# Edge attention on one core: the order of two matmuls, E and Q, in each batch of edges

## The chip, the cores and the metric

The kernel runs on one core of a Trainium2 chip. The time is the device time in microseconds (us) of one execution. The engines are named as in the profile: PE is TensorE (PEld its weight loads), DVE is VectorE, ACT is ScalarE, POOL is GpSimd and SP is the queue that issues plain transfers. They run side by side, each in the order of its own queue, and wait for each other through semaphores.

## The reference

A graph has 6250 nodes with 128 features each (8 heads of 16), and 206250 directed edges, sorted by destination node. Each edge has 128 features of its own.

```python
Qh, Kh, Vh = h @ WQ, h @ WK, h @ WV          # per node, seen as (N, 8, 16)
Eh = edge_attr @ WE                          # per edge
score = einsum('ehd,ehd,ehd->eh', Kh[src], Qh[dst], Eh) / sqrt(16)
score = exp(clip(score, -5, 5))
wV = segment_sum(Vh[src] * score[:, :, None], dst)
Z  = segment_sum(score, dst)
out = layernorm(x + wV / (Z[:, :, None] + 1e-6))
```

So every edge needs K and V of its source node, Q of its destination node and its own E.

## The kernel before

The edges are cut into 1612 tiles of 128, and the tiles into 406 batches: 401 of four tiles, and five small ones at the end. A short first part builds a table of K and V for all nodes in HBM (`kv`). The first 12 batches don't use it: they gather rows of x and project them themselves (`project`).

For each tile POOL issues one indirect DMA, which gathers 128 rows of 256 numbers (K and V of the sources) into `kvrows` (`gather`, L308 to L324). There are 15 buffers of one batch each. From batch 16 on, the first gather of a batch also waits for a matmul: `add_manual_dep` (L318 to L323) ties it to `expanded[b - lag(b)]`, which is the Q matmul of an earlier batch. The lag is 12 batches at first and falls by one every four batches to 1, which it reaches at batch 60 (L304 to L306).

Q of the destinations isn't gathered. Since the edges are sorted, a tile's destinations lie in a short window of nodes, and Q is spread to the edges by a matmul with a one-hot matrix (`qw`, in bfloat16 parts, times `onehotT`) into the PSUM tile `qps`. E comes from a float32 matmul of `we_sb` with the edge features `ea` into the PSUM tile `eps`. Both stand in `stage_a`. ACT copies `qps` to `qT` in SBUF, and DVE multiplies `qT` with `eps` to `eq` (`pairs`, L368). The PSUM pools of E and Q have one buffer each.

The stages of a batch are spread over several turns of the main loop (L481 to L533). In turn b the queues get, in this order:

- POOL: the gathers of batch b.
- PE: the four transposes of `eq` of batch b-1 into `pps` (`turn`, L376), then Q and E of batch b (`stage_a`), sometimes a block of nodes to finish (L412, L416), then `agg` of batch b-3 (`stage_c`, L441), sometimes a block of Q rows (L259).
- ACT: the copy of Q of batch b (L359), then the two exponentials of batch b-2 (L394, L396).
- DVE: `kq` of batch b-2 (L382, which needs its gathers landed), its reduction (L385) and clip (L388), `msg` of batch b-3 (L423), the one-hot matrices of batch b+2 (L343, L347), and `eq` of batch b (L368). Small operations of the layer norm are put between them (`fill`).
- SP: edge features (L295), destination rows (L285), windows of Q (L278), stores.

Until batch 12 the framework's scheduler orders the instructions. From batch 12 on the order is that of the code (`manual_schedule`, L482). At batch 60 the edges inside their windows are counted (L529, `count_inside`, with one small matmul, L200).

Of the kernel before, what the change touches and what calls it, by code (L numbers as in the profile page):

```python
# [8 lines left out]
F32 = mybir.dt.float32  # L9
# [6 lines left out]
P = 128  # L16
# [9 lines left out]
B = 4  # L26
# [54 lines left out]
def edge_attention(ctx: ExitStack, tc: tile.TileContext, x, xT, srcT, dstT, dstB, dst0, bnd, lo, eaT,  # L81
                   wq, wkv, we, out, kv, qtab, qs, relD):
    nc = tc.nc
# [14 lines left out]
    we_sb = cp.tile([D, D], F32, name="we_sb")  # L98
# [13 lines left out]
    with ExitStack() as fast:  # L112
# [94 lines left out]
        psE = fast.enter_context(tc.tile_pool(name="psE", bufs=1, space=bass.MemoryType.PSUM))  # L207
# [82 lines left out]
        def load_chunk(c):  # L290
            if c in chunks or c * CH >= NT:
                return
            n = min(CH, NT - c * CH) * P
            tl = ep.tile([P, CH * P], F32, name="ea")
            nc.sync.dma_start(tl[:, :n], eaT[:, c * CH * P:c * CH * P + n])  # L295
            chunks[c] = tl

        def ea_tiles(t, n):

            load_chunk(t // CH)  # L300
            j = t % CH * P
            return chunks[t // CH][:, j:j + n * P]
# [23 lines left out]
        def project(g, n):  # L326

            pt = psT.tile([P, B, P], F32, name="xtps", tag="oT")
            for i in range(n):
                nc.tensor.transpose(pt[:, i, :], g[:, i, :D], ident)  # L330
            xgT = wp.tile([P, B, P], F32, name="xgT", tag="kq", bufs=2)
            nc.scalar.copy(xgT[:, :n], pt[:, :n])
            for i in range(0, n, 2):
                k = min(2, n - i)
                pk = pair_bank(i // 2, "kvps", [P, 2, 2 * D])
                for j in range(k):
                    nc.tensor.matmul(pk[:, j, :], xgT[:, i + j, :], wkv_sb, start=True, stop=True)
                nc.scalar.copy(g[:, i:i + k, :], pk[:, :k, :])  # L338
# [12 lines left out]
        def stage_a(b, g):  # L351
            t0, n = batches[b][0], len(batches[b])
            if b < XB:
                project(g, n)
            oh, ohT = st8.pop(b)
            pq = psQ.tile([P, B * P], F32, name="qps")
            expanded[b] = nc.tensor.matmul(pq[:, :n * P], loaded[t0 // WT], ohT[:, :n * P], start=True, stop=True)  # L357
            qT = wp.tile([P, B * P], F32, name="qT", bufs=2)
            nc.scalar.copy(qT[:, :n * P], pq[:, :n * P])  # L359
            pe = psE.tile([P, B * P], F32, name="eps")  # L360
            nc.tensor.matmul(pe[:, :n * P], we_sb, ea_tiles(t0, n), start=True, stop=True)  # L361
            st8[b] = [n, g, oh, pe, qT]

        def pairs(b):
# [116 lines left out]
        for b in range(nbat + 4):  # L481
# [6 lines left out]
            if b < nbat:  # L488
                load_chunk(batches[b][0] // CH + EB - 3)
                load_rel(batches[b][0] // RC + 1)  # L490
                load_q(batches[b][0] // WT + QLOOK)
                g = gathered.pop(b) if b in gathered else gather(b)
                if b == min(XB, nbat - 1):
                    late_loads()
                if b == min(XB + 8, nbat - 1):
                    relative(C0, NT)
                if b == 14:
                    from_window(1)
                if b == 0:
                    for i in range(AHEAD):  # L500
                        stage_0(i)
                if b > 0:
                    turn(b - 1)
                stage_a(b, g)
            elif b == nbat:
                turn(b - 1)
# [184 lines left out]
```

## Time and profile before

| | us |
|---|---|
| median of 4 runs (lowest, highest) | 2044.31 (2042.33, 2045.83) |
| the profiled execution | 2045.63 |
| its span, first to last instruction | 2043.8 |
| busy in the span: PE, PEld | 1425.6, 993.9 |
| busy in the span: DVE, ACT, POOL | 1563.9, 473.7, 1533.3 |
| mean granted clock of TensorE | 0.886 |
| gathers on POOL: 1612, of which 1564 from the table | 0.951 each |

The profile comes from one execution. Its page has the busy time of each engine, the span in slices, the chain of work that ended last, and the costliest groups of instructions: line, engine, operation, output and inputs, count, then the total busy time and the mean of one in ns, then the idle time of the engine just ahead of them and what ended most of it. A timeline lists instructions in order: start in us, duration in us, engine, line and operation, and in brackets the idle time ahead of it with what ended it. Ends of matmuls are modelled, since they are pipelined. A float32 matmul shows as two rows (x2).

### The profile page before, as it was taken

What the parts mean: (1) busy time and instruction counts of PE and PEld (TensorE: products, weight loads), DVE (VectorE), ACT (ScalarE), POOL (GpSimd) and SP (SyncE); (2) the same over time, 40 slices, a digit from 0 to 9 for tenths busy, and PEclk for the clock granted to TensorE, in tenths of its full rate; (3) what the DMA queues carried; (4) which work ended last, traced back from release to release, by engine and by line L of the source; (5) the groups of instructions that cost most, each with busy time, mean ns of one, the idle gap of its engine ahead of it and who ended that gap; (6) DMA issues with size and microseconds to landing.
All of it is one profiled execution on the core that took longest, in us unless ns stands there. A gap on an engine that the chain in (4) does not pass through costs nothing.

```text
span 2043.8 us, 24333 instructions
## 1 busy us (share of the span) xinstructions
PE 1425.6 (70%) x6736; PEld 993.9 (49%) x6736; DVE 1563.9 (77%) x3542; ACT 473.7 (23%) x1548; POOL 1533.3 (75%) x1619
## 2 busy tenths in 40 slices
PE   6877876675767677766677676766776667666765
PEld 4655554453544445544444454544554444444444
DVE  3689998777778768777777777777878678777776
ACT  2422222222222222222222222221222222222221
POOL 7777777777777777777777777777777777777775
PEclk9989998989888988888888888888878888988888
DMA  9776766657666675656665666667565765666652
GB/s 297 226 229 194 226 197 212 195 174 211 192 196 184 186 212 171 205 174 190 210 189 174 199 203 197 183 188 217 167 201 174 207 203 179 195 182 199 202 169 81
DMA packets 177711, 398.12 MB, mean 195 GB/s; under 512 B 60988, under 2 KB 86758, under 8 KB 177568
## 3 DMA queue, kind: packets, MB, share of 16 engines
q0 software_dynamic: 76592, 208.18, 34.6%
q1 hardware_dynamic: 99836, 187.38, 29.3%
q8 instruction: 56, 0.92, 0.2%
q10 hardware_dynamic: 1140, 0.93, 0.1%
q14 instruction: 87, 0.71, 0.1%
HBM read 381.54 MB, written 14.81 MB: 194 GB/s over the span
## 4 chain that ended last, share of the span: by engine, by line
DMA 32%; DVE 26%; POOL 17%; issue 13%; PE 11%; ACT 1%; DVEq 0%; ACTq 0%; POOLq 0%; SPq 0%
DMA kvrows<-kv,src 30%; POOL kvrows L315 17%; DVE kq L382 7%; DVE sc L385 6%; PE agg L441 4%; DVE msg L423 3%; DVE eq L368 3%; PE eps L361 2%; DVE onehot L343 2%; PE pps L376 2%; DVE onehotT L347 1%; DVE sc L388 1%; DMA kv<-kvst 1%; PE finps L412 1%; PE qps L357 1%
## 5 line engine op out<-in xcount | busy, mean ns | idle before, releaser
L315 POOL DMA_INDIRECT kvrows<-kv,src x1564 | 1486.8, 951 | 478.1 <-issue 368.6
L441 PE MATMUL agg<-msg,onehot 128*128 128x136 f32 x3224 | 536.4, 316 | 518.4 <-DVE msg L423 420.9
L441 PEld LDWEIGHTS agg<-msg,onehot 128*128 128x128 f32 x3224 | 475.1, 217 | 833.7 <-issue 662.8
L382 DVE TENSOR_TENSOR kq<-kvrows,pps 128x512 f32<-128x512 f32 x406 | 275.5, 679 | 348.9 <-DMA kvrows<-kv,src 345.4
L361 PE MATMUL eps<-ea,we_sb 128*128 128x512 f32 (+1 forms) x812 | 469.5, 662 | 0.7 <-ACT kvrows L338 0.7
L359 ACT COPY qT<-qps 128x512 f32<-128x512 f32 x406 | 236.3, 582 | 540.7 <-PE qps L357 538.7
L376 PE MATMUL pps<-shift,eq 128*128 128x128 f32 x1612 | 299.7, 316 | 62.3 <-DVE eq L368 58.8
L368 DVE TENSOR_TENSOR eq<-qT,eps 128x512 f32<-128x512 f32 x406 | 272.9, 672 | 22.3 <-PE eps L361 19.7
L385 DVE TENSOR_REDUCE sc<-kq 128x32 f32<-128x512 f32 x406 | 276.0, 680 | 9.0
L423 DVE TENSOR_TENSOR msg<-kvrows,bank 128x512 f32<-128x512 f32 x406 | 274.1, 675 | 5.3 <-ACT bank L394 5.3
L343 DVE TENSOR_TENSOR onehot<-bank,dst_sb 128x512 f32<-128x512 f32 x406 | 274.5, 677 | 0.0
L394 ACT ACTIVATE bank<-sc 128x32 f32<-128x32 f32 x406 | 81.8, 201 | 822.5 <-DVE onehot L343 812.9
L376 PEld LDWEIGHTS pps<-shift,eq 128*128 128x128 f32 x1612 | 207.6, 159 | 118.9 <-DVE eq L368 114.1
L361 PEld LDWEIGHTS eps<-ea,we_sb 128*128 128x128 f32 x812 | 178.4, 221 | 28.6 <-ACT kvrows L338 3.4
L357 PE MATMUL qps<-onehotT,qw 126*128 126x512 bf16 x406 | 176.1, 434 | 0.9 <-ACT qT L359 0.9
L347 DVE TENSOR_SCALAR onehotT<-relb,node 126x512 bf16<-126x512 bf16 x406 | 152.4, 376 | 7.7 <-DMA relb<-relD 4.5
L388 DVE TENSOR_SCALAR sc<-sc 128x32 f32<-128x32 f32 x406 | 89.2, 220 | 9.0
L396 ACT ACTIVATE msg<-sc 128x32 f32<-128x32 f32 x406 | 86.6, 213 | 0.2
L315 POOL DMA_INDIRECT kvrows<-x,src x48 | 45.6, 951 | 16.4 <-issue 12.2
L454 ACT COPY sum<-agg 128x136 f32<-128x136 f32 x146 | 38.6, 265 | 35.6 <-PE agg L441 33.8
L357 PEld LDWEIGHTS <-qw 126*128 126x128 bf16 x406 | 44.5, 110 | 1.1 <-issue 0.9
L232 PE MATMUL kvacc<-wkv_sb,xT_sb 128*128 128x256 f32 (+1 forms) x98 | 29.3, 458 | 13.1 <-DMA xT_sb<-xT 5.4
(69 smaller groups left out, 474.3 us busy)
## 6 DMA issues: line engine op xcount, KB each, us to landing
ea<-eaT SPq DMA_DIRECT2D x201, 512.0 KB
relb<-relD SPq DMA_DIRECT2D x100, 504.0 KB
kvrows<-kv,src POOLq DMA_INDIRECT x1564
qw<-qs SPq DMA_DIRECT2D x202, 31.5 KB
kv<-kvst SPq DMA_DIRECT2D x12, 512.0 KB
qs<-qst SPq DMA_DIRECT2D x48, 96.0 KB
xb<-x SPq DMA_DIRECT2D x24, 128.0 KB
out<-h SPq DMA_DIRECT2D x24, 128.0 KB
```

Source lines behind the costliest of these rows:

```text
L315: ins = nc.gpsimd.indirect_dma_start(out=g[:k, i, :f], out_offset=None, in_=rows, in_offset=bass.IndirectOffsetOnAxis(ap=src_col(t)[:k], a ...
L343: nc.vector.tensor_tensor(oh[:, :n], iota_p[:, None, :].to_broadcast([P, n, P]), rel[:, t0:t0 + n, None].to_broadcast([P, n, P]), op=ALU.i ...
L347: nc.vector.tensor_scalar(ohT[:, :n * P], rels[t0 // RC][:, e0:e0 + n * P], node[:QROWS], None, op0=ALU.is_equal)
L357: expanded[b] = nc.tensor.matmul(pq[:, :n * P], loaded[t0 // WT], ohT[:, :n * P], start=True, stop=True)
L359: nc.scalar.copy(qT[:, :n * P], pq[:, :n * P])
L361: nc.tensor.matmul(pe[:, :n * P], we_sb, ea_tiles(t0, n), start=True, stop=True)
L368: nc.vector.tensor_tensor(eq[:, :n * P], qT[:, :n * P], pe[:, :n * P], op=ALU.mult)
L376: nc.tensor.transpose(pp[:, i, :], eq[:, i * P:i * P + P], ident)
L382: nc.vector.tensor_tensor(t1[:, :n], g[:, :n, :D], pp[:, :n], op=ALU.mult)
L385: nc.vector.tensor_reduce(sc[:, :n], t1[:, :n].rearrange("p b (h d) -> p b h d", h=H), axis=AX.X, op=ALU.add)
L423: nc.vector.tensor_tensor(m[:, :n, :D].rearrange("p b (h d) -> p b h d", h=H), g[:, :n, D:].rearrange("p b (h d) -> p b h d", h=H), exp_p[ ...
L441: nc.tensor.matmul(aggs[k], oh[:, i, :], m[:, i, :], start=first and not final, stop=last)
```

## The change

In `stage_a` the E matmul is issued ahead of the Q matmul instead of behind it. Nothing else differs. The copy of Q stays behind Q.

```diff
@@ stage_a
             oh, ohT = st8.pop(b)
+            pe = psE.tile([P, B * P], F32, name="eps")
+            nc.tensor.matmul(pe[:, :n * P], we_sb, ea_tiles(t0, n), start=True, stop=True)
             pq = psQ.tile([P, B * P], F32, name="qps")
             expanded[b] = nc.tensor.matmul(pq[:, :n * P], loaded[t0 // WT], ohT[:, :n * P], start=True, stop=True)
             qT = wp.tile([P, B * P], F32, name="qT", bufs=2)
             nc.scalar.copy(qT[:, :n * P], pq[:, :n * P])
-            pe = psE.tile([P, B * P], F32, name="eps")
-            nc.tensor.matmul(pe[:, :n * P], we_sb, ea_tiles(t0, n), start=True, stop=True)
             st8[b] = [n, g, oh, pe, qT]
```

With the lines moved, E is line 357, Q line 359 and the copy line 361 in the changed kernel; the others keep their numbers.

## The prediction

> **What bounds the kernel now.** I read the page from the top, and its first part misleads. No engine is over 77% busy, and the chain that ended last hops between DMA, DVE and POOL. So I went to the costliest groups, and asked of each what ended its idle time.
>
> ```profile
> PE 1425.6 (70%) x6736; PEld 993.9 (49%) x6736; DVE 1563.9 (77%) x3542; ACT 473.7 (23%) x1548; POOL 1533.3 (75%) x1619
> ...
> L315 POOL DMA_INDIRECT kvrows<-kv,src x1564 | 1486.8, 951 | 478.1 <-issue 368.6
> ...
> L382 DVE TENSOR_TENSOR kq<-kvrows,pps 128x512 f32<-128x512 f32 x406 | 275.5, 679 | 348.9 <-DMA kvrows<-kv,src 345.4
> ...
> L368 DVE TENSOR_TENSOR eq<-qT,eps 128x512 f32<-128x512 f32 x406 | 272.9, 672 | 22.3 <-PE eps L361 19.7
> ```
>
> The gather row tells it: 1564 gathers of 0.95 us with 478.1 us of idle time, which is 0.30 us for each. POOL therefore starts a gather every 1.25 us and does nothing else. The timeline of POOL alone confirms it: 1612 gathers run from 3.61 to 2027.51 us, 2023.9 us for 1611 steps, median step 1.25. Only 11.6 us of that lies above 1.25 per step. What follows the last gather (2027.5 to 2043.8, 16.3 us) is DVE's row of small operations and one store. So **POOL's stream of gathers is the kernel's clock**. DVE idles 345.4 us for gathers that have not landed. The wait the change is aimed at, DVE's product eq for TensorE's E (L361), is 19.7 us in 31 pieces on an engine with that much to spare.
>
> The one thread from the edit back to POOL is the pace wait (L318 to L325). From batch 16 on, the first gather of batch b waits for the Q matmul of batch b-lag(b); the lag falls from 12 to 1 at batch 60 and stays there. I set each batch's first gather beside the end of that Q matmul, from the timelines of POOL and PE. A gather that waits starts 0.28 us behind the end of Q. Two do so in this execution, batch 25 and batch 28. This is the first:
>
> ```profile
> 128.05 0.95 POOL L315 DMA_INDIRECT kvrows<-kv,src  x1 [0.30 <-issue]
> ...
> 129.49 0.63 PE L357 MATMUL qps<-onehotT,qw 126*128 126x512 bf16 x1
> ...
> 129.92 1.19 PE L361 MATMUL eps<-ea,we_sb 128*128 128x512 f32 x2
> ...
> 130.16 0.58 ACT L359 COPY qT<-qps 128x512 f32<-128x512 f32 x1 [2.58 <-PE qps L357]
> 130.40 0.94 POOL L315 DMA_INDIRECT kvrows<-kv,src  x1 [1.40 <-PE qps L357]
> ```
>
> Q of batch 15 ends at 130.12, E at 131.11 (129.92 + 1.19), and POOL starts batch 25 at 130.40, 1.1 us late. Time lost there is lost for good, since POOL never has room to catch up.
>
> **The change, part by part.** It removes and adds no instruction that computes. The built order of the two programs differs on PE only from batch 12 on (in the first 12 the scheduler puts E and Q in the same places), and there E stands ahead of Q. On DVE 394 products wait for ACT alone instead of PE and ACT. On SP 190 loads of edge features lose a wait on PE. ACT and POOL keep their order and their waits.
>
> *Freed wait on DVE.* The trace has 394 semaphore instructions of 21 ns ahead of eq, 8.3 us in all, on DVE's queue. Where DVE runs without a gap eq starts with no idle time ahead of it, so they are covered by the operation before. I take 0; the other end is ten batches between 15 and 25 at 21 ns, 0.2 us earlier.
>
> *Freed wait on SP.* E of a batch ended at most 1.7 us behind its Q, and a reload of Q's weights for the same batch still waits for that Q, which now ends last. The loads go out at the same time: 0. Q in turn now stands behind E's wait for its features; E sat idle 0.7 us in all, none of it for a load, so 0 again.
>
> *eq's operands.* Before, eq is ready when E ends (warm: Q's start + 1.24; the copy ends 0.24 earlier). After, the pair still takes 1.24 us, but the copy follows it: 0.04 to start and 0.58 to run. So eq is ready 0.6 us later than now. In a run of batches without a DMA wait eq starts 1.1 to 1.3 us after E's end, so 0.6 is hidden; 71 of 389 eq start within 0.75 us of it, and DVE loses up to 0.6 there. Behind a waiting eq stand kq, the reduction and msg of older batches, and behind msg TensorE's agg. So the wait that was removed is replaced by a longer one. Nearly all of it disappears into the 345.4 us for which DVE waits for gathers anyway.
>
> *The gather's release.* This is the part on the path. Q is now done when E was done: 0.86 us later in the median of batches 12 to 400, up to 1.72 where the clock was low. Subtracting that and 0.28 from the room of every first gather from batch 16, three of 390 turn clearly negative (batch 32 stands at 0.02, with what POOL lost before it to spare):
>
> - Batch 25 waits for Q of 15: Q ends at 131.11 instead of 130.12, **+0.99 us**.
> - Batch 28 waits for Q of 19, which ended at 145.45 and E at 146.31: 0.86 later by itself. It is later still by eq of batches 15 and 18, both of which started within 0.11 us of E's end and now wait some 0.5 us each for the copy. That is 1.4 to 1.9, of which 0.99 is already in POOL's stream: **+0.4 to +0.9**.
> - Batch 62 waits for Q of 61, which sits behind the counting of line 530:
>
> ```profile
> 316.72 0.63 PE L357 MATMUL qps<-onehotT,qw 126*128 126x512 bf16 x1
> ...
> 317.14 1.91 PE L361 MATMUL eps<-ea,we_sb 128*128 128x512 f32 x2
> ...
> 318.31 0.94 POOL L315 DMA_INDIRECT kvrows<-kv,src  x1 [0.30 <-DVE msg L423]
> ```
>
> Here Q ends at 317.35, E at 319.05, and the gather starts at 318.31. The gather would start at 319.05 + 0.28 = 319.33, **+1.02**. DVE had last waited for a gather at batch 57, so what POOL lost before shifts both sides alike.
>
> Unknown is whether E in front exposes its weight load: Q's takes 0.10, one of E's 0.2, so 0 to 0.1 us at each of the three, 0 to 0.3. Below nothing is excluded because the pair's matmuls are the same.
>
> After batch 63 the lag is one and the room is wide: counted with E already in front, its median is 5.6 us, its least inside the run 0.41 (batch 277). The last two batches have 0.66 and -0.01, which the shift of POOL's stream leaves about where it is. The tail hangs on kq at 2020.35, which waits for a gather, and shifts with it.
>
> Sum: 0.99 + 0.65 + 1.02 + 0.15 = **+2.8 us** (2.4 to 3.2). The profiled execution took 2045.63 us (span 2043.8), which gives 2048.4. The median of the four runs is 2044.31, 1.3 below that execution, so the median forecast is **2047.1 us**, +0.14%. This kernel's runs spread from 2042.33 to 2045.83, and a difference within 0.2% (4.1 us) is about what can't be told from none.
>
> [...] The rows show two lengths of the same matmul: Q 0.38 and 0.63 us, with E's end 0.86 and 1.70 behind it, and PEclk between 0.8 and 1.0. [...] With all three places slow the sum would be 3 x 1.70 = 5.1 us, an estimate, against 2.8 by the rows; I keep the rows, where one place was slow throughout, one in part, and one not.
>
> **Rivals.**
> 1. *It does nothing measurable for POOL* (0 to +1.5 us, 2044 to 2046). For it: 387 of 390 waits have room. It needs batches 15, 19 and 61 to fall better by luck. Against: batches 25 and 28 are at the wait already, so any lateness of Q there goes straight in. Chance 0.18.
> 2. *Slower: the pace wait binds in the steady state.* Place: the lag-one waits from batch 60. Mechanism: eq is late by 0.6 after a stall, then the transposes, then E and Q, and the lateness X reaches the next release on top of E. With X taken from the room of all 346 lag-one waits, the loss is 2.3 us at X = 0.5, 5.2 at 1.0, 11.7 at 1.5. Part of it is batch 62's own, 1.02 + X. With the 1.6 to 2.2 us of the ramp the total passes 4.1 from X of about 0.5, which is where it decides; the median would be 2051.4 at X = 1.0 and 2058 at 1.5. For it: 46 eq start within 0.2 us of E's end. Against: the narrow waits come right after a stall, where eq had been ready long before. Chance 0.20.
> 3. *Faster.* What POOL lost to Q is 1.1 us at batch 25 and 0.3 at 28. If the freed semaphore waits brought the ramp forward by all of it, the median would be 2042.9. I see no source for 4 us, since 2012 of 2044 us are POOL's own pitch. Chance of over 0.2% faster 0.03, of a smaller gain 0.04.
>
> **How the numbers follow.** The forecast (+1.5 to +4.1) has 0.55, rival 1 0.18, rival 2 0.20, rival 3 0.07 in its two parts. Faster by over 0.2% is 0.03, slower by over 0.2% 0.20, and the rest, 0.55 + 0.18 + 0.04, is 0.77. The range runs from 2043.3, which is rival 1's lower end less the scatter of a median, to 2052.0, which takes in rival 2 up to X of about 1.0; about 0.17 is left out.
>
> **What would show it.** In the profile after, POOL's mean gather stays at 951 ns with 0.30 us ahead of it. Gathers of batches 25, 28 and 62 show idle time put down to PE qps, and the last gather starts 2 to 3 us later. ACT's copy starts about 0.86 us later in each batch against the transposes. eq's idle time is put down to ACT's copy and is larger than 22 us, some 40 to 70, and DVE's wait for gathers is smaller by about as much. I am wrong if POOL's idle time rises over many batches past 60 (rival 2), or if POOL's last gather moves and none of the three places does.

## The result, and the profile after

The changed kernel takes 2046.63 us (median of 32 runs, 2042.41 to 2049.96), the kernel before 2044.43 us (52 runs, 2042.18 to 2047.50). The ratio is 1.0011, with a 95% interval of 1.0006 to 1.0015: slower by 1.2 to 3.1 us, clear of the noise, but inside the 0.2% that the prediction calls hard to tell from none. The forecast was 2047.1, +2.8 us. The profiled execution of the changed kernel took 2049.32 us, that of the kernel before 2045.63.

The page of the changed kernel, the lines that answer to those shown of before (line, engine, operation, count, then busy us, mean ns, idle us ahead and what ended most of it):

```profile
span 2047.5 us, 23810 instructions
...
PE 1428.0 (70%) x6736; PEld 954.1 (47%) x6736; DVE 1563.2 (76%) x3542; ACT 467.4 (23%) x1548; POOL 1532.8 (75%) x1619
...
L315 POOL DMA_INDIRECT kvrows<-kv,src x1564 | 1485.1, 950 | 482.6 <-issue 374.4
...
L382 DVE TENSOR_TENSOR kq<-kvrows,pps 128x512 f32<-128x512 f32 x406 | 275.3, 678 | 330.3 <-DMA kvrows<-kv,src 327.6
...
L368 DVE TENSOR_TENSOR eq<-qT,eps 128x512 f32<-128x512 f32 x406 | 273.1, 673 | 45.7 <-ACT qT L361 43.8
```

Two columns are to be compared. eq's idle time is now put down to the copy and is 43.8 us instead of 19.7 for E, and DVE's wait for gathers is 327.6 instead of 345.4: it fell by 17.8, so about three quarters of the 24.1 that eq waits longer were paid out of the old wait. And POOL's gathers cost the same (950 ns), but its idle time ahead of the table's gathers rose from 478.1 to 482.6 us. That 4.5 is what POOL lost in this execution by waiting. The span rose by less, 3.7 us (2043.8 to 2047.5), since the gathers themselves took 0.5 us less in all and the work behind the last one 0.3 less. POOL's timeline says where the waiting lies. The gathers of batches 25, 28, 32 and 62, with E and Q of batches 15 and 19 ahead of the first two, and E, Q and the copy of batch 61 ahead of the last:

```profile
129.96 1.92 PE L357 MATMUL eps<-ea,we_sb 128*128 128x512 f32 x2
131.66 0.44 PE L359 MATMUL qps<-onehotT,qw 126*128 126x512 bf16 x1
...
132.38 0.94 POOL L315 DMA_INDIRECT kvrows<-kv,src  x1 [1.67 <-DMA kvrows<-kv,src]
...
147.16 1.02 PE L357 MATMUL eps<-ea,we_sb 128*128 128x512 f32 x2
148.02 0.38 PE L359 MATMUL qps<-onehotT,qw 126*128 126x512 bf16 x1
...
148.67 0.94 POOL L315 DMA_INDIRECT kvrows<-kv,src  x1 [1.48 <-PE qps L359]
...
170.38 0.94 POOL L315 DMA_INDIRECT kvrows<-kv,src  x1 [1.35 <-PE qps L359]
...
320.66 1.92 PE L357 MATMUL eps<-ea,we_sb 128*128 128x512 f32 x2
...
322.37 0.63 PE L359 MATMUL qps<-onehotT,qw 126*128 126x512 bf16 x1
...
323.04 0.58 ACT L361 COPY qT<-qps 128x512 f32<-128x512 f32 x1 [9.21 <-PE qps L359]
323.27 0.94 POOL L315 DMA_INDIRECT kvrows<-kv,src  x1 [2.57 <-DVE onehotT L347]
```

Take the last line: Q ends at 323.00, and POOL starts 0.27 us later after 2.57 us of idle time. The profile names DVE there, but the distance to Q's end is the one that every gather has that waits for Q (0.27 or 0.28). The gather at 132.38, which names a transfer, has it as well: Q of batch 15 ended at 131.66 + 0.44 = 132.10, 0.28 earlier. The profile infers the releaser; where two events lie close, the constant distance is the better witness.

I call idle time of POOL ahead of a gather beyond its usual 0.30 us a **pause**. Adding up all pauses of the profiled executions, one of each kernel, gives the table that the rest rests on:

| kernel | E first in | gathers tied to | pauses, us (batch: size) | sum |
|---|---|---|---|---|
| before | none | Q | 25: 1.10, 28: 0.29 and 0.27 on its second gather | 1.7 |
| changed | 12 to the end | Q | 25: 1.37, 28: 1.18 and 0.28, 32: 1.06, 62: 2.26 | 6.2 |
| e1_late | 64 to the end | Q | none | 0.0 |
| e2_ramp | 12 to 63 | Q | 25: 5.30, 28: 0.11 and 0.28, 32: 0.84, 62: 1.03, 405: 0.16 | 7.7 |
| e3_release_e | none | E | 25: 1.05, 28: 0.33 and 0.27, 62: 1.03, one of 0.25 elsewhere | 2.9 |
| e4_after_turn | 12 to the end | transposes | 28: 0.15 and 0.27, 62: 1.37 | 1.8 |

### The profile page after: what moved, and what is told of

It reads as the page before. It is cut to its first block, busy times and chain, and to the rows that moved or that the text cites. A ratio compares the mean times of both kernels' runs of the same rounds, so it can differ in the third digit from the quotient of the medians.

```text
span 2047.5 us, 23810 instructions
## 1 busy us (share of the span) xinstructions
PE 1428.0 (70%) x6736; PEld 954.1 (47%) x6736; DVE 1563.2 (76%) x3542; ACT 467.4 (23%) x1548; POOL 1532.8 (75%) x1619
## 4 chain that ended last, share of the span: by engine, by line
DMA 29%; DVE 26%; POOL 17%; PE 13%; issue 12%; ACT 2%; DVEq 0%; SPq 0%; ACTq 0%; POOLq 0%
DMA kvrows<-kv,src 27%; POOL kvrows L315 17%; DVE kq L382 6%; DVE sc L385 6%; PE agg L441 4%; DVE msg L423 4%; PE eps L357 3%; DVE eq L368 3%; PE pps L376 2%; DVE onehot L343 2%; DVE sc L388 2%; DVE onehotT L347 2%; DMA kv<-kvst 1%; PE finps L412 1%; PE qps L359 1%
## 5 line engine op out<-in xcount | busy, mean ns | idle before, releaser
L315 POOL DMA_INDIRECT kvrows<-kv,src x1564 | 1485.1, 950 | 482.6 <-issue 374.4
L441 PEld LDWEIGHTS agg<-msg,onehot 128*128 128x128 f32 x3224 | 468.7, 214 | 765.6 <-issue 649.6
L382 DVE TENSOR_TENSOR kq<-kvrows,pps 128x512 f32<-128x512 f32 x406 | 275.3, 678 | 330.3 <-DMA kvrows<-kv,src 327.6
L357 PE MATMUL eps<-ea,we_sb 128*128 128x512 f32 (+1 forms) x812 | 477.4, 674 | 0.7 <-ACT kvrows L338 0.7
L368 DVE TENSOR_TENSOR eq<-qT,eps 128x512 f32<-128x512 f32 x406 | 273.1, 673 | 45.7 <-ACT qT L361 43.8
L359 PE MATMUL qps<-onehotT,qw 126*128 126x512 bf16 x406 | 167.2, 412 | 0.7 <-ACT qT L361 0.7
L357 PEld LDWEIGHTS eps<-ea,we_sb 128*128 128x128 f32 x812 | 145.0, 223 | 3.4 <-ACT kvrows L338 3.4
L232 PE MATMUL kvacc<-wkv_sb,xT_sb 128*128 128x256 f32 (+1 forms) x98 | 29.2, 456 | 14.7 <-DMA xT_sb<-xT 5.5
```

What stands on the lines that cost most here:

```text
L315: ins = nc.gpsimd.indirect_dma_start(out=g[:k, i, :f], out_offset=None, in_=rows, in_offset=bass.IndirectOffsetOnAxis(ap=src_col(t)[:k], a ...
L368: nc.vector.tensor_tensor(eq[:, :n * P], qT[:, :n * P], pe[:, :n * P], op=ALU.mult)
L382: nc.vector.tensor_tensor(t1[:, :n], g[:, :n, :D], pp[:, :n], op=ALU.mult)
L441: nc.tensor.matmul(aggs[k], oh[:, i, :], m[:, i, :], start=first and not final, stop=last)
```

## The experiments

**The theories.** *Release*: all of the loss is POOL's, at the pace wait, because Q now ends when E did; it happens only in the ramp of the lag and at the counting of batch 60. *Product*: DVE's product waits longer for a copy behind a later Q, and that costs a little in every batch.

Runs e1 to e4 shared a chip on which the kernel before took 2049.01 us (33 runs); the changed kernel itself has no run there. With 11 runs each their ratios are good to 0.9 parts in a thousand, about 1.8 us, so most medians only lean one way or the other, and the pauses have to decide. They come from one execution each, and not always a usual one: the profiled executions of e1 (2044.15 us) and e3 (2045.02) were the fastest of their 11, some 5 us below their medians, and no profile shows where the others lost those 5 us.

**e1_late and e2_ramp: the place.** One edit, with the condition turned round for the second:

```diff
+            e_first = b >= 64            # e2_ramp: b < 64
+            if e_first:
+                pe = ...; E matmul
             pq = ...; Q matmul; copy
+            if not e_first:
+                pe = ...; E matmul
```

> E ahead of Q from batch 64 on only; batches 12 to 63 keep Q ahead of E. Release theory (the time is lost where a gather waits for a Q that now ends when E did, and that happens only in the ramp, batches 25 to 62): 2044.4 us like the kernel before, within 0.7, with pace waits at batches 25 and 28 alone. Product theory (the time is lost a little in every batch, because VectorE's product now waits for the copy behind a later Q): 343 of 394 batches have it, so 0.87 of 2.2 us, 2046.3.

> The complement: E ahead of Q in batches 12 to 63 only. Release theory: all of the loss, 2046.6 us, with waits for Q at batches 25, 28, 32 and 62 as in the changed kernel. Product theory, spread over all batches: 52 of 394 batches, 2044.7.

e1 took 2049.24 us, ratio 1.0004 (0.9995 to 1.0013); e2 took 2051.02, ratio 1.0010 (1.0001 to 1.0019). The ratios lean as the release theory has it, but e1's interval holds both forecasts. Its profile says more. Who waited for whom on DVE in e1 (total us, times, longest; by the edit the copy is L363 there and eq L373):

```profile
DVE kq L387 <- DMA kvrows<-kv,src: 319.7, 149, 5.9
DVE eq L373 <- ACT qT L363: 45.9, 53, 1.5
```

The product waits for the copy just as in the changed kernel (45.9 us against 43.8), in 342 batches with E in front, and POOL doesn't pause once. That execution's span, 2042.4 us, is the shortest of all profiles here. So from batch 64 on the later product costs POOL nothing. I had expected pauses at batches 25 and 28 in e1, as in the kernel before; there were none, and the reason is in the last section. e2 has the pauses at 25, 28, 32 and 62, and hardly one after; its 5.30 at batch 25 is larger than anything the order explains, also for that reason.

**e3_release_e and e4_after_turn: the mechanism.** e3 keeps the old order and makes only the release late; e4 keeps the new order and takes the release away from E and Q:

```diff
# e3, on the kernel before
-            expanded[b] = nc.tensor.matmul(pq...)
+            nc.tensor.matmul(pq...)
-            nc.tensor.matmul(pe...)
+            expanded[b] = nc.tensor.matmul(pe...)
# e4, on the changed kernel: the Q matmul as above, and in turn()
-                nc.tensor.transpose(pp[:, i, :], ...)
+                expanded[b + 1] = nc.tensor.transpose(pp[:, i, :], ...)
```

> Q ahead of E as before, so the product and the copy keep their times, but the gathers are tied to the E matmul instead of the Q matmul: the release comes late and nothing else does. Release theory: +0.99 at batch 25, +0.86 at batch 28 of which 0.99 is already lost, +1.02 at batch 62: 2046.4 us, and less than the changed kernel at batch 28, where the copy's lateness added. Product theory: 2044.4.

> E ahead of Q as in the changed kernel, but the gathers are tied to the transposes that stand just ahead of the pair, so that the release no longer waits for E or Q; the product is as late as in the changed kernel. Release theory: batch 25 is released about 0.6 us earlier than in the kernel before and batch 62 doesn't wait; what is left is the copy's lateness of about 0.5 at batch 28: 2044.0 us, within 0.8. Product theory: 2046.6, like the changed kernel.

e3 took 2049.87 us, ratio 1.0009 (1.0000 to 1.0018); e4 took 2048.66, ratio 0.9998 (0.9989 to 1.0007). Both medians lie where the release theory puts them. The product theory has e4 at 1.0011, outside its interval, and e3 at 1.0000, on the edge of its own. In e3 the places that are free of the copy's lateness are batches 25 and 62, and POOL paused 1.05 and 1.03 us there:

```profile
128.56 0.63 PE L357 MATMUL qps<-onehotT,qw 126*128 126x512 bf16 x1
128.99 1.39 PE L361 MATMUL eps<-ea,we_sb 128*128 128x512 f32 x2
...
130.65 0.95 POOL L315 DMA_INDIRECT kvrows<-kv,src  x1 [1.35 <-PE eps L361]
...
316.62 1.91 PE L361 MATMUL eps<-ea,we_sb 128*128 128x512 f32 x2
...
318.81 0.94 POOL L315 DMA_INDIRECT kvrows<-kv,src  x1 [1.32 <-DVE onehotT L347]
```

E of batch 15 ends at 130.38 and the gather starts 0.27 later. Tied to Q, which ended at 129.19, it would have been released at 129.46, ahead of its turn at 129.60, so all of the 1.05 us is the late release. (The forecast of 0.99 was on top of the 1.10 us of the kernel before; this execution reached batch 15 earlier and had no such pause to add to.) E of batch 61 ends at 318.53, and the gather of batch 62 starts 0.28 later: 1.03 against 1.02 forecast. In e4 batch 25 doesn't pause, as expected, and batch 28 pauses 0.15, where about 0.5 was expected. But batch 62 pauses 1.37 us, and I had expected none. There the release is the transposes of batch 60, and they are late:

```profile
308.73 1.92 PE L357 MATMUL eps<-ea,we_sb 128*128 128x512 f32 x2
...
310.44 0.63 PE L359 MATMUL qps<-onehotT,qw 126*128 126x512 bf16 x1
...
311.11 0.59 ACT L361 COPY qT<-qps 128x512 f32<-128x512 f32 x1 [3.76 <-PE qps L359]
...
311.73 0.69 DVE L368 TENSOR_TENSOR eq<-qT,eps 128x512 f32<-128x512 f32 x1 [0.79 <-ACT qT L361]
...
318.03 1.11 PE L376 MATMUL pps<-shift,eq 128*128 128x128 f32 x4
319.42 0.95 POOL L315 DMA_INDIRECT kvrows<-kv,src  x1 [1.67 <-PE pps L376]
```

E of batch 60 took 1.92 us, with a granted clock of 0.50 from 308.7 to 310.6, Q and the copy followed, and eq of batch 60 waited 0.79 us. Behind eq on DVE stands the counting of batch 60, and behind that the small matmul that holds TensorE (L200 at 317.91, after 5.77 us of idle time). So at this place a late product passes straight on, because DVE has no gather wait to absorb it in.

Pauses aren't the whole of an execution's time. e4's span, 2047.2 us, is almost that of the changed kernel (2047.5), although POOL paused 4.4 us less. Its gathers took longer, by 3 ns on average:

```profile
L315 POOL DMA_INDIRECT kvrows<-kv,src x1564 | 1490.1, 953 | 478.6 <-issue 369.5
```

That is 5.0 us more than in the changed kernel (1485.1). Whether the edit or the execution makes them longer isn't shown. So what e4 shows of the mechanism is where POOL waits, and its 11 runs show that the whole comes out at the time of the kernel before.

**e5 to e12: a different bound.** These eight fell on two other chips, on which the kernel before itself takes 2428.22 us (e5 to e8) and 2432.07 us (e9 to e12). The expectations of e11 and e12 put that down to gathers that land slowly. The traces don't show it: in e10 a gather keeps POOL busy for the same 951 ns, and the packets of the gathers' queue took as long in all (29.2% of 2429.2 us of 16 engines, against 34.6% of 2043.8 before). What is slower there stays open. In the profile of e10, which differs from the kernel before in its ramp alone, POOL pauses for 386 us in all. Differences of 2 us can't be read from them, so the forecasts for them are not tested as they were meant. The edits:

```diff
# e5 (on before), e6 (on the changed kernel), e12 (as e5): no pace wait
-                if i == 0 and b >= LOCK:
-                    made = expanded[b - lag(b)]
# e7, e11, on the changed kernel: the Q matmul untied as in e3, and in stage_c()
+                expanded[b + 3] = nc.tensor.matmul(aggs[k], ...)
# e8, on the changed kernel
-            return max(STEP, 12 - (b - LOCK) // 4)
+            return max(STEP + 1, 13 - (b - LOCK) // 4)
# e9 (on the changed kernel), e10 (on before)
+            return max(STEP, 13 - (b - LOCK) // 4)
```

> The kernel before without the pace wait: gathers wait for nothing but a free buffer, 15 batches back, and the earlier gathers' landing. Release theory: POOL loses what it now loses at batches 25 and 28, 1.7 us in the profiled execution, 0 to 2 in others: ratio to the kernel before 0.9992. If the pace wait does work of its own (keeps gathers from crowding other transfers), it is slower than before.

> The changed kernel without the pace wait; the product is as late as in the changed kernel, but nothing ties a gather to Q. Release theory: no pause is left and the order of E and Q costs nothing, the same time as the kernel before without the pace wait, within 0.7 us: ratio to the kernel before 0.9992. Product theory: 2.2 us above the kernel before without the pace wait.

> A dose: the changed kernel with the gathers tied to agg, the last matmuls of the same turn, 2.1 us after the end of Q in the median of the changed kernel's profile. Subtracting these ends from the starts of the first gathers there, 34 of the lag-one waits after batch 60 have no room, 24 us together, and in the ramp batch 24 lacks 3.6. Release theory: pauses all through the steady state, 15 to 27 us above the changed kernel, 2062 to 2074 us where that one takes 2046.6. Product theory, in which the release doesn't matter: like the changed kernel.

> The changed kernel with every lag one batch longer (13 falling to 2): the gather of a batch waits for the Q matmul one batch earlier, 3.6 to 5 us sooner. Release theory: no pause at batches 25, 28, 32 or 62, the time of the kernels without the pace wait, ratio to the kernel before 0.9992. Product theory: like the changed kernel, 1.001.

> The changed kernel with the ramp of the lag begun one batch longer (13, falling by one every four batches to 1 at batch 64), so that batches 16 to 63 are released one batch earlier and the steady state keeps its lag of 1. Release theory: no pause for Q at batches 25, 28, 32 and 62, the time of the kernel before less its own pauses there: ratio to the kernel before 0.9985 to 1.000, against 1.0011 of the changed kernel. If the loss sits in the steady state or in the later product: 1.001.

> The kernel before with the same longer ramp. Release theory: the same time as the changed kernel with the longer ramp, within 0.7 us, and 0 to 2 us under the kernel before. If the order of E and Q costs something away from the release, this one is 2 us under the changed kernel with the longer ramp.

> The dose again, gathers tied to agg of the same turn, to be read where gathers land as fast as in the profiles of the kernel before and the changed kernel. Release theory: pauses all through the steady state, 15 to 27 us above the changed kernel, ratio to the kernel before 1.008 to 1.014. If the release doesn't matter: 1.001.

> The kernel before without the pace wait, again to be read where gathers land fast. Where they landed slowly it took 1.12 of the kernel before. If what hurt there was gathers running ahead of the other loads, it can happen only where TensorE falls behind POOL's stream; here TensorE has 6.5 us of room, and POOL's stream is the bound: ratio 0.999 to 1.01. If the pace wait protects the other loads here as well: above 1.02.

| run | order | release | median us | ratio to before on its chip |
|---|---|---|---|---|
| e5_before_free | Q first | none | 2717.32 | 1.1209 (1.1179 to 1.1239) |
| e6_after_free | E first | none | 2721.57 | 1.1209 (1.1189 to 1.1229) |
| e12_before_free | Q first | none | 2715.43 | 1.1162 (1.1129 to 1.1195) |
| e7_after_agg | E first | agg | 2432.33 | 1.0014 (1.0001 to 1.0027) |
| e11_after_agg | E first | agg | 2436.15 | 1.0015 (0.9999 to 1.0030) |
| e8_after_lag1 | E first | Q, lag + 1 | 2451.08 | 1.0079 (1.0056 to 1.0103) |
| e9_after_ramp13 | E first | Q, longer ramp | 2455.69 | 1.0094 (1.0076 to 1.0113) |
| e10_before_ramp13 | Q first | Q, longer ramp | 2431.18 | 0.9998 (0.9988 to 1.0008) |

Two things can be read. Without a tie between gathers and Q, no cost of the order shows: e5 and e6 have the same ratio, though with intervals of 0.2 to 0.3% (5 to 7 us) a cost of 2 us would not. And on these chips the pace wait earns its place: without it the kernel takes 12% longer. Who POOL waits for in e5 (its kernel is two lines shorter, so msg is L421):

```profile
POOL kvrows L315 <- DVE msg L421: 571.4, 124, 7.7
POOL kvrows L315 <- issue: 434.3, 1409, 1.2
```

A gather that waits for msg waits for a free buffer, so POOL has run all 15 buffers ahead. What that does to the other transfers isn't shown. ACT's copy waits in e5 815.2 us for something the profile can't name, but it does so for 779.6 us in e9 too, which keeps the pace wait.

e9 against e10 is a failure of my expectation. With the same longer ramp I expected both orders within 0.7 us; there they are 24.5 us apart. So on these chips the order costs more than 2 us when the release is Q. The changed kernel itself has no run there, so how much of that the changed kernel pays, and why, stays open. The release theory as it stands doesn't explain it: with E in front, the kernels tied to agg, a later release, took 1.0014 and 1.0015 of the kernel before, and those tied to an earlier Q than the changed kernel's took 1.0079 and 1.0094. The dose (e7, e11) is inconclusive for the same reason: POOL isn't the bound, and a later release can't show what it takes from a bound POOL.

## Why the prediction was right

*The bound.* Right. 1612 gathers at a step of 1.25 us make up the time. What moves it by a few us is the pauses of that stream and the length of the gathers themselves (e4).

*The freed waits on DVE and SP, taken at 0.* Nothing contradicts it: in e1 they are freed from batch 64 on, no stretch of POOL's stream got shorter than its step, and a gain of 0.2 us can't be seen.

*eq is 0.6 us later, and it is absorbed.* Right over the whole run (eq's waits 43.8 us, forecast 40 to 70; DVE's wait for gathers smaller by 17.8), but not in the ramp, where it counts. The 345.4 us of gather waits that were to absorb it don't reach there. Between 111 and 325 us, batches 12 to 61, DVE waits for no gather in the kernel before nor, by the same view, in the changed one; the first wait is that of batch 66. (The prediction's "last waited for a gather at batch 57" isn't in this profile.) DVE's waits of eq from 111 to 325 us, in the kernel before, then in the changed kernel, and the first gather wait of the kernel before:

```profile
DVE eq L368 <- ACT msg L396: 1.3, 2, 1.0
DVE eq L368 <- PE eps L361: 0.8, 3, 0.4
...
DVE eq L368 <- ACT qT L361: 6.1, 6, 1.6
...
349.93 0.69 DVE L382 TENSOR_TENSOR kq<-kvrows,pps 128x512 f32<-128x512 f32 x1 [6.24 <-DMA kvrows<-kv,src]
```

So the products of the ramp waited 6.1 us instead of 2.1, in the changed kernel at batches 12, 15, 18, 21, 60 and 61. The prediction charged two of these, 15 and 18, with 0.5 us each; they waited 1.30 and 0.97 (0.23 and 0.43 in the kernel before). In e4 they waited 5.0 us, and with the release taken from E and Q POOL paused only at 28 and 62. So the late product and the late release cost time together, at the same few gathers.

*The three places of the release.* Batches 25, 28 and 62 paused, as forecast, and so did batch 32. The sizes are another matter. Between the two profiles the pauses grew by 0.27 us at batch 25 (0.99 forecast), 0.9 at 28 (0.4 to 0.9), 1.06 at 32 (nothing) and 2.26 at 62 (1.02). At 25 the release itself came later than forecast, since E of batch 15 took 1.92 us instead of 1.19, but POOL's own stream was also 1.7 us later there (its turn for batch 25 came at 131.01 instead of 129.30). Batch 32 stood at 0.02 us of room and was let off "with what POOL lost before it to spare". But E and Q of batch 24, which release it, had fallen back further than POOL: they began at 168.87 instead of 165.72, 3.15 us later, and POOL's turn for batch 32 came only 2.08 later. That the late products of batches 12 to 21 held them back fits, but no run isolates it. At 62, e3 shows that the release alone is 1.03, and e2, with E in front and a fast E of batch 60, has the same 1.03. The other 1.2 comes with eq of batch 60, late by a slow E and the copy in the changed kernel and in e4; I had charged such lateness at batch 28 and not here.

*The sum.* The profiled pair differs in its pauses by 4.5 us (6.2 less 1.7), against 2.8 forecast. The medians differ by 2.2 us, interval 1.2 to 3.1. The profiled execution of the changed kernel took 2049.32 us, above all but one of the 32 runs, so its pauses may well be above the usual. The forecast fits the median better than its own parts fit that one execution: the cause and the places were foreseen, but that 2.8 comes so near to 2.2 is in part luck, with one part too large, one missing and one less than half of what was measured.

*The clock.* E of batch 60 took 1.02 us in before, e1, e2 and e3, 1.91 us in the changed kernel and 1.92 in e4. The granted clock was 1.00 while it ran in before (307.3 to 308.3) and 0.50 in the changed kernel (310.5 to 312.3). Of the three profiles with E ahead of Q at that batch (e2, the changed kernel, e4) it was slow in two, and of the three with Q ahead in none. So the order alone doesn't decide it; whether it makes a slow E likelier, six profiles can't tell. The pause at batch 62 is 1.03 (e2) or 2.26 by it. At the three places, batches 15, 19 and 61, E took 1.19, 1.02 and 1.91 us in the kernel before and 1.92, 1.02 and 1.92 in the changed kernel. The prediction's 5.1 us was an estimate for all three slow; that occurred in neither profile. What lowers the granted clock at these places isn't shown.

*The rivals.* Rival 1 had batches 15, 19 and 61 fall better by luck: e1, whose ramp is that of the kernel before, shows that such luck occurs, for it has no pause at all. Rival 2, the steady state, didn't happen: room for the first gather after Q fell from a median of 6.5 to 5.3 us from batch 60 on, and in the two profiles in which E is in front there and Q releases (the changed kernel, e1) POOL never paused after batch 62. The least room there was 0.6 and 0.3 us, so it was not far off.

## What to carry to other kernels

Before an edit on an engine with idle time, find the engine whose stream never pauses, and list every wait that ties it to the edited code; then subtract the edit's delay from the room of each such wait, one by one. A mean of room says nothing: 6.5 us in the median and none at two batches. And where two orders of the same work free different waiters, ask which waiter sits on the bound: here the product gained a simpler wait that nobody needed, and the gathers lost 0.86 us or more that four of them needed. And look for the slack where the critical wait stands: DVE's 345 us of waiting for gathers lay behind the ramp, and the ramp had none of it.

## What was not expected

**The pause at batch 25 measures the start.** The DVE product of batch 11, before the order of E and Q differs at all, started at 108.69 us in e1, 109.14 in e3, 111.28 in before, 110.98 in the changed kernel and 114.66 in e2. The pauses at batch 25 are 0, 1.05 (tied to E), 1.10, 1.37 and 5.30. POOL's own stream varies much less there: its turn for batch 25 came between 129.30 and 131.01 in these five. So whatever the first 110 us lose beyond what the lag of the ramp covers goes into the total. This is likely part of why runs of one kernel spread over 5 us, though one profile of each kernel can't show it, and it blurs any edit whose effect lies in the ramp. A longer ramp (e10) was meant to take that out; on its chip it gave 0.9998, and on a chip like that of e1 it wasn't tried.

**One gather is stretched by a DVE operation.** In the kernel before, the gather at 148.50 us took 2.09 us instead of 0.95, next to DVE's subtraction of L178 (148.09, 1.68 us); another took 1.32 beside L147 and L148. In the changed kernel and in e1 to e4 a gather that starts while L178 runs takes between 1.30 and 2.43 us. In all six profiles it ends 0.82 or 0.83 us behind the end of L178, however long it had run, while a gather that starts 0.06 us ahead of L178 keeps its 0.95 (the changed kernel, e2, e3). So it is L178 that holds the gather up. Such stretches add to POOL's stream like pauses.
